# ScalarE instead of VectorE empties two PSUM banks of a deformable-convolution kernel

## The chip, the cores and the metric

The kernel runs on one core of a Trainium2 chip. The metric is the device time of one execution in microseconds, as the median of several runs. A core has five engines that run side by side and meet at semaphores: TensorE (PE in the profile) multiplies matrices into PSUM, VectorE (DVE) and ScalarE (ACT) do elementwise work and can read PSUM, GpSimd (POOL) does elementwise work on SBUF and issues transfers, SyncE (SP) issues transfers. Each engine works through its own list of instructions in order. All data here is float32.

## The reference

The input is 32 images of 96 x 56 x 56. Two layers follow each other.

Layer 0 is an inverted residual: a 1x1 convolution to 576 channels, batch norm and SiLU, a depthwise 3x3 convolution, batch norm and SiLU, a squeeze-and-excite gate, a 1x1 convolution back to 96 channels, batch norm, and the input added.

Layer 1 weighs its input by a channel attention and a spatial attention, both made from spectra and pooled statistics, and gets `y`. Then it computes, with `aux` made of `y`, coordinates and a resized spectrum:

```python
offset = _conv(aux, off_w, off_b, (1, 1))
gate = jax.nn.sigmoid(_conv(jax.nn.relu(_conv(aux, dg1_w, dg1_b, (1, 1))), dg2_w, dg2_b))
y_base = _conv(y, base_w, base_b, (1, 1))
...
sampled = _grid_sample_taps(y, px, py)
y_def = jnp.einsum('bcthw,oct->bohw', sampled, def_w.reshape(c, c, 9))
y_def = y_def + def_b[None, :, None, None]
z = (1 - gate) * y_base + gate * y_def
mu = z.mean((0, 2, 3), keepdims=True)
var = ((z - mu) ** 2).mean((0, 2, 3), keepdims=True)
...
return jax.nn.relu(zn + x)
```

`px` and `py` are the pixel's place plus the offsets of nine taps, and `_grid_sample_taps` samples bilinearly there. `zn` is `z` normalised over all images by `mu` and `var`.

## The kernel before

Layer 1 works in bands of 8 rows (448 pixels), seven per image, 224 in all. A band is made in two halves of seven tiles. Sampling is done by matrix products: for each 4 x 4 tile an 8 x 8 block of `y` is transposed (`block_channels`: GpSimd copies the blocks at L721, PE transposes at L725, ScalarE copies the result out at L727) and multiplied with a matrix of bilinear weights (`sample_tiles`: PE at L739, ScalarE copies to `v` at L743). `pack` (L750) copies the last two of the nine taps to the upper partitions on ScalarE, so that `deform` (L758) needs seven products per half. The products of both halves of a band go to one PSUM bank of a pool of its own, `pd`, with a single buffer. All other banks come from a pool of six, `mm` (a seventh, `acc`, serves small things).

`joint_conv` makes, in one bank of `mm`, the gate's hidden rows, the 18 rows of offsets and a third of the base convolution (nine products at L615); ScalarE empties the hidden rows (L635) and the base rows (L637), and the rest of the base convolution follows in another bank (L644, emptied at L649). `offsets` takes the offsets' rows out of the first bank with two copies, L664, to the tile `at`. GpSimd stores `at` to memory (L672), VectorE takes its largest magnitude (L676), SyncE loads it back spread over partitions, ScalarE turns it to weights (L687, L689), and VectorE multiplies row and column weights (`weights`, L710).

`end_half` issues the products of a half and, two slots after the second half, `join`: `combine` reads the `pd` bank and makes `z` with three VectorE steps (L797 to L799) and its statistics (L800); the store to memory (L1061, GpSimd) is issued seven slots later.

Beside a band, the generators of the other work are advanced by a fixed plan of slots (`pump`): layer 0 of the image after next (`hidden`: PE at L169, ScalarE at L173, and the depthwise convolution on VectorE, nine steps of up to 1568 columns at L260 and L262, then SiLU on ScalarE at L222), and projection and attention of the next image (among it the spectra: PE at L396 and L420, ScalarE at L423 and L427, VectorE's sums `m_fe` and `m_fy` at L437, and PE's products of these at L440). SyncE's list stands in the order of the program. On the other engines a scheduler places the instructions by its own estimate of times, so that a change of an engine can move others. After the last band `normalise` (L1347, L1349) runs through all of `z` once more. There is a second way of sampling for large offsets, `gather_block`, which also calls `combine`; the profile has no instruction of it.

Of the kernel before, what the change touches and what calls it, by code (L numbers as in the profile page):

```python
# [9 lines left out]
AF = mybir.ActivationFunctionType  # L10
ALU = mybir.AluOpType
# [5 lines left out]
C, H, W = 96, 56, 56  # L17
# [18 lines left out]
BW = NBW  # L36
TS = 4
NTX = W // TS
# [79 lines left out]
def bank(p):  # L118
    return p["mm"].tile([128, 512], FP, name="mm")
# [509 lines left out]
def joint_conv(nc, p, yp, j, hid):  # L629


    w = p["w"]
    pa = bank(p)
    conv3(nc, pa[:, :BW], w["joint"], yp, CJ, j)
    nc.scalar.activation(hid, pa[:DMID, :BW], AF.Relu, bias=w["dg1b"][:DMID])  # L635
    yb = p["yb"].tile([C, BW], FP, name="yb")
    nc.scalar.activation(yb[BC:], pa[OFF0 + QC :, :BW], AF.Identity, bias=w["cv"]("base_b")[BC:])  # L637
    yield yb, pa[OFF0 : OFF0 + NOFF, :BW]
    pb = bank(p)
    for k in range(NTAP):  # L640
        dy, dx = divmod(k, 3)
        r0 = j * RB + dy + PD - 1
        for i in range(2):
            nc.tensor.matmul(pb[i * BC : (i + 1) * BC, : BW // 2].rearrange("p (h w) -> p h w", h=RB // 2), w["base"][:, k],  # L644
                             yp[:C, r0 + i * RB // 2 : r0 + (i + 1) * RB // 2, dx + PD - 1 : dx + PD - 1 + W],
                             start=(k == 0), stop=(k == NTAP - 1))
    yield
    for i in range(2):
        nc.scalar.activation(yb[:BC, i * BW // 2 : (i + 1) * BW // 2], pb[i * BC : (i + 1) * BC, : BW // 2], AF.Identity,  # L649
                             bias=w["cv"]("base_b")[:BC])  # L650
    yield


def offsets(nc, p, yp, j, top, hid, ybs, hds, defer):

    w = p["w"]
    joint = joint_conv(nc, p, yp, j, hid)
    yb, pa = next(joint)  # L660
    ybs.append(yb)
    at = p["off"].tile([NOFF, NTX, 2, TP], FP, name="at")
    for s in range(2):
        nc.vector.tensor_copy(at[:, :, s].rearrange("o t (r c) -> o t r c", r=TS),  # L664
                              pa[:, s * BW // 2 : (s + 1) * BW // 2].rearrange("o (r t c) -> o t r c", r=TS, t=NTX))
    yield
    yield
    next(joint)
    yield
    od = p["dp"].tile([NTX, 2, NOFF, TP], FP, name="od")  # L670
    p["tc"].keep_in_program_order(
        nc.gpsimd.dma_start(od.rearrange("t s o p -> o (t s) p"), at.rearrange("o t s p -> o (t s) p")))  # L672
    next(joint)
    yield
    next(joint, None)
    nc.vector.tensor_reduce(top, at.rearrange("o t s p -> o (t s p)"), AX.X, ALU.max, apply_absolute_value=True)  # L676
    for _ in range(7):
        yield
    ht = p["ht"].tile([SB * NTX, 4, KP], FP, name="ht")
    src = od.rearrange("t s o p -> t (s o p)").unsqueeze(0).to_broadcast([SB, NTX, 4 * KP])  # L680
    nc.sync.dma_start(ht.rearrange("q n k -> q (n k)"), src)
    for _ in range(3):
        yield

    def hats():
        ho = p["ht"].tile([SB * NTX, 2, 2, KP], FP, name="ho")
        p["tc"].keep_in_program_order(nc.scalar.activation(  # L687
            ho.rearrange("q x s n -> q s x n"), ht.rearrange("q (s x) n -> q s x n", s=2), AF.Abs, bias=w["blk"]))
        nc.scalar.activation(ho, ho, AF.Relu, bias=w["one"], scale=-1.0)  # L689
        hd = p["dp"].tile([2, 2, SB, NTX, KP], FP, name="hd")  # L690
        nc.scalar.dma_start(hd.rearrange("x s i t n -> (i t) (x s) n"), ho.rearrange("q x s n -> q (x s) n"))
        hds.append(hd)

    defer(hats)
# [68 lines left out]
def gate_of(nc, p, hid):  # L763

    pg = bank(p)
    nc.tensor.matmul(pg[:C, :BW], p["w"]["dg2"], hid, start=True, stop=True)
    return gate_from(nc, p, pg)
# [17 lines left out]
def base_conv(nc, p, j, yp):  # L785

    pb = bank(p)
    conv3(nc, pb[:C, :BW], p["w"]["base"], yp, C, j)
    yb = p["q1"].tile([C, BW], FP, name="yb")
    nc.scalar.activation(yb, pb[:C, :BW], AF.Identity, bias=p["w"]["cv"]("base_b"))  # L790
    return yb


def combine(nc, p, j, pd, yb, gate, st):

    z = p["q2"].tile([C, BW], FP, name="z")
    nc.vector.scalar_tensor_tensor(z, pd[:C, :BW], p["w"]["cv"]("def_b"), yb, ALU.add, ALU.subtract)  # L797
    nc.vector.scalar_tensor_tensor(z, gate, 1.0, z, ALU.add, ALU.mult)
    nc.vector.scalar_tensor_tensor(z, z, 0.5, yb, ALU.mult, ALU.add)  # L799
    nc.vector.bn_stats(st[:, j], z)  # L800
    return z
# [152 lines left out]
def layers(tc, a, dp, x1d, zd, stats, far):  # L954
# [6 lines left out]
    nc = tc.nc  # L961
    B = x1d.shape[0]
    with ExitStack() as ctx:
        p = {"tc": tc, "dp": ctx.enter_context(tc.tile_pool(name="l1d", bufs=3, space=DRAM))}
# [3 lines left out]
        yp, = padded(nc, p, a, 1)  # L968
# [21 lines left out]
        streams, later = [], []  # L990
        slot = 0
# [68 lines left out]
        def store(b, j, z):  # L1060
            nc.gpsimd.dma_start(zd[b][:, j * BW : (j + 1) * BW], z)  # L1061

        def join(n, pd, gate, st):
            b, j = bands[n]
            z = combine(nc, p, j, pd, ybs[n], gate, st)
            later.append((slot + 7, lambda: store(b, j, z)))
            if j == NBD - 1:
                nc.vector.bn_aggr(stats[:, b], st)

        def end_half(n, h, v, gate, st):  # L1070
            if h == 0:
                pds[n] = p["pd"].tile([128, 512], FP, name="pd")
            deform(nc, p, pds[n], v, h)
            if h:
                pd = pds.pop(n)
                later.append((slot + 2, lambda: join(n, pd, gate, st)))

        ends, pds = [], {}

# [9 lines left out]
        hids, gates, ybs, hds, ready = [], [], [], [], []  # L1089
# [31 lines left out]
        for n, (b, j) in enumerate(bands):  # L1121
            if j == 0:
                st = p["st"].tile([C, NBD, 6], FP, name="st")
# [7 lines left out]
            for h in range(2):  # L1131
                v = p["vp"].tile([128, NTAP, NTH, 2, TP], FP, name="v")
                prepare(2 * n + h + READY + AHEAD)
                s = ready.pop(0)
# [17 lines left out]
                if h == 0:  # L1152
                    if n % 2 == 0:
                        gates.extend(gates_of(nc, p, hids[n // 2]))
                    gate = gates.pop(0)
# [108 lines left out]
def gather_block(tc, a, dp, x1d, zd, stats):  # L1264

    nc = tc.nc
    B = x1d.shape[0]
    sd = dp.tile([B, C, 2], FP, name="sd")
    with ExitStack() as ctx:
        p = {"dp": ctx.enter_context(tc.tile_pool(name="l1d", bufs=1, space=DRAM))}  # L1270
        pools(tc, ctx, p, PSUM, (("mm", 7), ("acc", 1)))
        constants(tc, ctx, a, p, True)
        yp, = padded(nc, p, a, 1)
        table = dp.tile([TAB, 4 * C], FP, name="table")
        with tc.tile_pool(name="l1z", bufs=1) as zp:
            zt = zp.tile([116, TAB * C // 116], FP, name="zt")
            nc.gpsimd.memset(zt, 0.0)
            tz = table.rearrange("(p n) f -> p (n f)", p=116)
            for i in range(4):
                nc.sync.dma_start(tz[:, i * zt.shape[1] : (i + 1) * zt.shape[1]], zt)  # L1280
        pools(tc, ctx, p, None, (("ca", 1), ("s1p", 1), ("xc", 2), ("sp", 1), ("sq", 2), ("hq", 1), ("q1", 2), ("q2", 2),
                                 ("hid", 2), ("off", 1), ("ix", 2), ("vp", 1), ("gp", 4), ("smp", 2)))
        with tc.For_i(0, B, 1) as b:
            st = p["sp"].tile([C, NBD, 6], FP, name="st")
            zo = p["dp"].tile([C, HW], FP, name="zo")
            xi = p["dp"].tile([C, HW], FP, name="xi")
            nc.sync.dma_start(xi.unsqueeze(0), x1d[bass.ds(b, 1)])
            for _ in attend(tc, p, 0, None, None, None, xi, True):
                pass
            for q in range(NB):  # L1290
                attend_table(nc, p, yp, table, xi, q)
            load_freq(nc, p, yp, 0, 0, H)
            for j in range(NBD):
                hid, wq, idx = locate(nc, p, yp, j)
                v = p["vp"].tile([C, NTAP, BW], FP, name="v")
                for t in range(GT):
                    sample_table(nc, p, table, wq, idx, v, t)
                pd = bank(p)
                for k in range(NTAP):
                    nc.tensor.matmul(pd[:C, :BW], p["w"]["def"][:, k], v[:, k], start=(k == 0), stop=(k == NTAP - 1))  # L1300
                z = combine(nc, p, j, pd, base_conv(nc, p, j, yp), gate_of(nc, p, hid), st)
                nc.sync.dma_start(zo[:, j * BW : (j + 1) * BW], z)
            mv = p["sp"].tile([C, 2], FP, name="mv")
            nc.vector.bn_aggr(mv, st)
            nc.sync.dma_start(zd[bass.ds(b, 1)], zo.unsqueeze(0))
            nc.sync.dma_start(sd[bass.ds(b, 1)].rearrange("o c n -> (o c) n"), mv)
    nc.sync.dma_start(stats, sd.rearrange("b c s -> c b s"))
# [209 lines left out]
```

## Time and profile before

| | us |
|---|---|
| median of 3 runs (lowest, highest) | 9049.27 (9045.97, 9068.44) |
| the profiled execution's own time | 9059.03 |
| span of the profiled execution | 9057.2 |
| PE busy | 8175.3 |
| VectorE busy | 7184.4 |
| ScalarE busy | 5393.5 |
| GpSimd busy | 2902.8 |

The page gives busy time per engine, the span in 40 slices (each digit is the busy share in tenths), the costliest groups of instructions by source line, and, behind the bar, the idle time of the engine just before the instructions of a group with what ended it. The view of waits adds these idle times up by engine, line and releaser. A matmul in float32 is recorded as two. PEclk is the clock that TensorE was granted, as a share of full speed; its mean over the execution was 0.939. In the slices of the middle the load is even: image follows image, one every 263 us or so.

### The profile page before, as it was taken

The numbers are of one execution on the slowest core, as the hardware profiler recorded it, in microseconds if no ns is written. First come the engines' busy times: TensorE is split into PE (matmuls) and PEld (weight loads), VectorE is DVE, ScalarE is ACT, GpSimd is POOL, SyncE is SP. The second block draws the span as 40 slices with busy tenths as digits, with TensorE's granted clock in tenths as the row PEclk, the third lists the DMA queues.
The fourth block names the chain that finished last, engine by engine and source line by source line (L and its number), as shares of the span: only waits on it lengthen the run. The fifth ranks groups of instructions, "written<-read, shape, count | busy, mean of one in ns | idle before, by whom it ended". The sixth has DMA issues, their size and how long they took to land. (4 is left out here: it accounts for less than half of the span.)

```text
span 9057.2 us, 137476 instructions
## 1 busy us (share of the span) xinstructions
PE 8175.3 (90%) x52406; PEld 5193.5 (57%) x52406; DVE 7184.4 (79%) x6629; ACT 5393.5 (60%) x10486; POOL 2902.8 (32%) x2800
## 2 busy tenths in 40 slices
PE   5889999999999999999999999999999999999960
PEld 3456565665656566565656656565665655566640
DVE  7688888888888888888888888888888888888333
ACT  2356665666666666666666666666666666666553
POOL 0233333333333333333333333333333333333210
PEclk9889999999999999999999999999999999999985
DMA  2356666666666666666666666666666666666669
GB/s 82 108 142 160 163 169 165 157 154 153 163 166 171 166 157 147 158 165 164 172 161 154 159 157 168 165 174 161 154 154 160 165 166 172 166 156 144 144 188 416
DMA packets 1068758, 1486.48 MB, mean 164 GB/s; under 512 B 590191, under 2 KB 839839, under 8 KB 1055807
## 3 DMA queue, kind: packets, MB, share of 16 engines
q1 hardware_dynamic: 858995, 985.20, 46.4%
q10 hardware_dynamic: 153803, 329.80, 10.2%
q0 software_dynamic: 55296, 162.60, 6.7%
q8 instruction: 420, 6.88, 0.4%
q14 instruction: 244, 1.99, 0.1%
HBM read 1064.29 MB, written 412.65 MB: 163 GB/s over the span
## 5 line engine op out<-in xcount | busy, mean ns | idle before, releaser
L262 DVE SCALAR_TENSOR_TENSOR acch<-hp,w,acch 128x1512 f32<-128x1512 f32 (+1 forms) x2250 | 4456.4, 1981 | 141.4 <-ACT hp L173 103.8
L615 PE MATMUL mm<-yp,c_jointW 104*128 104x448 f32 x4032 | 1679.6, 568 | 10.1 <-DMA yp<-fqd 10.1
L758 PE MATMUL pd<-v,c_def 128*96 128x224 f32 (+1 forms) x6272 | 1468.8, 382 | 142.7 <-DVE z L797 115.6
L721 POOL COPY ybl<-yp 96x448 f32<-96x448 f32 x896 | 1048.3, 1198 | 1204.9 <-PE mm L725 1204.8
L758 PEld LDWEIGHTS pd<-v,c_def 128*96 128x96 f32 (+1 forms) x6272 | 1062.2, 176 | 449.8 <-issue 116.9
L615 PEld LDWEIGHTS mm<-yp,c_jointW 104*128 104x128 f32 x4032 | 776.6, 196 | 784.2 <-issue 747.4
L743 ACT COPY v<-mm 96x288 f32<-96x288 f32 (+1 forms) x2688 | 1004.3, 441 | 156.0 <-PE mm L739 109.3
L169 PE MATMUL mm<-xt,w 96*128 96x392 f32 (+3 forms) x2688 | 1058.5, 527 | 35.3 <-DMA xt<-in_x 33.1
L739 PE MATMUL mm<-wc,yt 64*96 64x144 f32 x12544 | 1056.9, 300 | 20.8 <-DVE sq L379 6.7
L739 PEld LDWEIGHTS mm<-wc,yt 64*96 64x96 f32 x12544 | 834.2, 164 | 317.3 <-issue 199.1
L173 ACT ACTIVATE hp<-mm,sh,inv 128x392 f32<-128x392 f32 (+2 forms) x1216 | 810.7, 673 | 344.8 <-PE mm L169 290.5
L710 DVE TENSOR_TENSOR wc<-wc,wr 128x1008 f32<-128x1008 f32 x448 | 566.6, 1265 | 412.5 <-DMA wr<-hd 385.1
L644 PE MATMUL mm<-yp,c_base0W 96*64 96x224 f32 x8064 | 830.1, 358 | 5.7 <-ACT hp L173 5.7
L329 PE MATMUL mm<-hq,w3s 128*96 128x392 f32 x2048 | 749.7, 510 | 63.6 <-DMA hq<-h2d 62.2
L672 POOL DMA_DIRECT2D od<-at x224 | 186.7, 834 | 1908.3 <-DVE at L664 1292.6
L750 ACT COPY v<-v 32x448 f32<-32x448 f32 x1344 | 755.1, 562 | 29.7
L727 ACT COPY yt<-mm 128x384 f32<-128x384 f32 (+1 forms) x896 | 353.9, 439 | 700.7 <-PE mm L725 699.0
L644 PEld LDWEIGHTS mm<-yp,c_base0W 96*64 96x64 f32 x8064 | 555.2, 135 | 282.7 <-issue 61.0
L635 ACT ACTIVATE hid<-mm,c_dg1b 50x448 f32<-50x448 f32 x224 | 140.8, 628 | 868.4 <-PE mm L615 858.4
L476 POOL TENSOR_TENSOR o<-o,xc 96x392 f32<-96x392 f32 x256 | 376.2, 1470 | 806.2 <-ACT o L339 804.2
L222 ACT ACTIVATE acch<-acch,sh,inv 128x1568 f32<-128x1568 f32 x288 | 488.4, 1696 | 202.8 <-DVE acch L262 176.5
L329 PEld LDWEIGHTS mm<-hq,w3s 128*96 128x96 f32 x2048 | 323.0, 166 | 395.2 <-issue 367.5
(194 smaller groups left out, 9325.3 us busy)
## 6 DMA issues: line engine op xcount, KB each, us to landing
h2d<-acch ACTq DMA_DIRECT2D x288, 784.0 KB
wc<-hd SPq DMA_DIRECT2D x896, 252.0 KB
wr<-hd SPq DMA_DIRECT2D x448, 504.0 KB
hq<-h2d SPq DMA_DIRECT2D x128, 980.0 KB
hq<-h2d SPq DMA_DIRECT2D x128, 784.0 KB
hq<-x1d SPq DMA_DIRECT2D x768, 98.0 KB
ht<-od SPq DMA_DIRECT2D x224, 252.0 KB
hd<-ho ACTq DMA_DIRECT2D x224, 252.0 KB
```

What stands on the lines that cost most here:

```text
L169: nc.tensor.matmul(pt[p0 : p0 + w1.shape[1], : rows * W], w1, xts[hf][:, r0 * W : (r0 + rows) * W], start=True, stop=True)
L173: nc.scalar.activation(h1[lo:hi, row0 : row0 + rows, 1 : 1 + W], pt[lo:hi, : rows * W].rearrange("p (h w) -> p h w", h=rows), AF.Silu, bia ...
L262: nc.vector.scalar_tensor_tensor(acc[:, lo:hi], win, wk, acc[:, lo:hi], ALU.mult, ALU.add)
L329: nc.tensor.matmul(pts[half][:C, :EW], w3s[:, ch], hq, start=(i == 0), stop=False)
L615: nc.tensor.matmul(view, weights[:, k], yp[:channels, r0 : r0 + RB, dx + PD - 1 : dx + PD - 1 + W], start=(k == 0), stop=(k == NTAP - 1))
L644: nc.tensor.matmul(pb[i * BC : (i + 1) * BC, : BW // 2].rearrange("p (h w) -> p h w", h=RB // 2), w["base"][:, k], yp[:C, r0 + i * RB // 2 ...
L710: p["tc"].keep_in_program_order(nc.vector.tensor_tensor(wc, wc, wr, ALU.mult))
L721: nc.gpsimd.tensor_copy(yb[:, :, s], blocks)
L739: nc.tensor.matmul(pt[k][:C, (t - lo) * KP : (t - lo + 1) * KP], yt[ps, t], s[ps, t * KP : (t + 1) * KP], start=True, stop=True)
L743: nc.scalar.copy(v[:C, :, lo:hi, k].rearrange("c k t p -> c t k p"), pt[k][:C, : (hi - lo) * KP].rearrange("c (t k p) -> c t k p", t=hi - ...
L750: nc.scalar.copy(v[C:, 1 + 2 * i : 3 + 2 * i], v[i * QC : (i + 1) * QC, KA:])
L758: nc.tensor.matmul(out.rearrange("c q (t x) -> c t q x", x=TS), p["w"]["def"][ks, k], v[ks, k].rearrange("c t s (r x) -> c t (s r) x", r=T ...
```

## The change

Both places in which VectorE reads the results of layer 1 out of PSUM go to ScalarE.

The two copies of the offsets' rows (L664) become ScalarE copies of the same rows to the same tile. The first step of `combine`, which added the bias to the `pd` bank and subtracted the base convolution in one instruction, is split in two: a new function `take` copies the bank to `z` on ScalarE and adds the bias on the way, and `combine` begins with a subtraction on VectorE that reads and writes `z` in SBUF. `take` is called in `end_half` directly after the products of the second half, two slots before `join`; what `join` gets is `z`, not the bank. `gather_block` is changed in the same way.

```diff
     at = p["off"].tile([NOFF, NTX, 2, TP], FP, name="at")
     for s in range(2):
-        nc.vector.tensor_copy(at[:, :, s].rearrange("o t (r c) -> o t r c", r=TS),
-                              pa[:, s * BW // 2 : (s + 1) * BW // 2].rearrange("o (r t c) -> o t r c", r=TS, t=NTX))
+        nc.scalar.copy(at[:, :, s].rearrange("o t (r c) -> o t r c", r=TS),
+                       pa[:, s * BW // 2 : (s + 1) * BW // 2].rearrange("o (r t c) -> o t r c", r=TS, t=NTX))
...
-def combine(nc, p, j, pd, yb, gate, st):
+def take(nc, p, pd):
 
     z = p["q2"].tile([C, BW], FP, name="z")
-    nc.vector.scalar_tensor_tensor(z, pd[:C, :BW], p["w"]["cv"]("def_b"), yb, ALU.add, ALU.subtract)
+    nc.scalar.activation(z, pd[:C, :BW], AF.Identity, bias=p["w"]["cv"]("def_b"))
+    return z
+
+
+def combine(nc, p, j, z, yb, gate, st):
+
+    nc.vector.tensor_tensor(z, z, yb, ALU.subtract)
     nc.vector.scalar_tensor_tensor(z, gate, 1.0, z, ALU.add, ALU.mult)
     nc.vector.scalar_tensor_tensor(z, z, 0.5, yb, ALU.mult, ALU.add)
     nc.vector.bn_stats(st[:, j], z)
...
-        def join(n, pd, gate, st):
+        def join(n, z, gate, st):
             b, j = bands[n]
-            z = combine(nc, p, j, pd, ybs[n], gate, st)
+            combine(nc, p, j, z, ybs[n], gate, st)
...
             if h:
-                pd = pds.pop(n)
-                later.append((slot + 2, lambda: join(n, pd, gate, st)))
+                z = take(nc, p, pds.pop(n))
+                later.append((slot + 2, lambda: join(n, z, gate, st)))
```

More of the change, by code (lines that the diff above doesn't have):

```diff
@@ L1300, in gather_block @@
                     nc.tensor.matmul(pd[:C, :BW], p["w"]["def"][:, k], v[:, k], start=(k == 0), stop=(k == NTAP - 1))
-                z = combine(nc, p, j, pd, base_conv(nc, p, j, yp), gate_of(nc, p, hid), st)
+                z = take(nc, p, pd)
+                combine(nc, p, j, z, base_conv(nc, p, j, yp), gate_of(nc, p, hid), st)
                 nc.sync.dma_start(zo[:, j * BW : (j + 1) * BW], z)
```

## The prediction

> **What bounds the kernel now.** I read the page first (busy times, slices), then the waits of TensorE, then the groups of the moved lines, then the timeline around two gaps with the clock in narrow windows.
>
> ```profile
> span 9057.2 us, 137476 instructions
> PE 8175.3 (90%) x52406; PEld 5193.5 (57%) x52406; DVE 7184.4 (79%) x6629; ACT 5393.5 (60%) x10486; POOL 2902.8 (32%) x2800
> PE   5889999999999999999999999999999999999960
> ```
>
> From slice 4 to slice 38 PE is busy in nine tenths or more of every slice, and DVE in eight tenths. PE is the bound; what it still loses are waits, and this view lists them (who waited for what: us, times, longest):
>
> ```profile
> PE pd L758 <- DVE z L797: 115.6, 26, 6.1
> PE acc L440 <- DVE m_fy L437: 72.8, 30, 5.6
> PE acc L440 <- DVE m_fe L437: 71.1, 31, 2.5
> PE mm L725 <- DVE at L664: 57.2, 28, 5.7
> PE pd L758 <- ACT v L743: 19.3, 36, 2.8
> ```
>
> The first and the fourth row are what the change touches: about once per image PE stands before the next band's deformable products because VectorE has not yet emptied the single pd bank, and once before the transposes because the offsets' rows still hold a bank. The groups of the two lines, and of ScalarE's like-sized work:
>
> ```profile
> L797 DVE SCALAR_TENSOR_TENSOR z<-pd,c_cvec,yb 96x448 f32<-96x448 f32 x224 | 152.2, 679 | 170.3 <-PE pd L758 166.1
> L664 DVE COPY at<-mm 18x224 f32<-18x224 f32 x448 | 156.6, 380 | 201.8 <-ACT yb L637 197.8
> L637 ACT ACTIVATE yb<-mm,c_cvec 32x448 f32<-32x448 f32 x224 | 140.5, 627 | 4.1
> L649 ACT ACTIVATE yb<-mm,c_cvec 64x224 f32<-64x224 f32 x448 | 198.2, 443 | 320.7 <-PE mm L644 317.9
> ```
>
> One z gap, from the timeline, and the clock around it (the number before the last two columns is PEclk):
>
> ```profile
> 1040.09 6.78 DVE L262 SCALAR_TENSOR_TENSOR acch<-hp,w,acch 128x1568 f32<-128x1568 f32 x3
> 1042.71 1.74 ACT L750 COPY v<-v 32x448 f32<-32x448 f32 x3
> 1046.90 0.68 DVE L797 SCALAR_TENSOR_TENSOR z<-pd,c_cvec,yb 96x448 f32<-96x448 f32 x1
> 1047.64 1.06 PE L758 MATMUL pd<-v,c_def 96*96 96x224 f32 x2 [4.65 <-DVE z L797]
> ...
> 1043.00:1047.60 4.60, 0.00 (x0) 0.00 (x0) 4.48 (x4) 3.96 (x8) 0.00 (x0) 0.74 1.03 297
> 1047.60:1052.00 4.40, 4.36 (x14) 3.50 (x15) 4.25 (x8) 0.48 (x1) 0.52 (x1) 0.50 0.94 197
> 1052.00:1060.00 8.00, 8.00 (x61) 6.39 (x61) 5.48 (x7) 6.34 (x14) 1.06 (x2) 1.00 0.91 152
> ```
>
> The pd bank was full since 1037.9; z stood behind three 2 us steps of the first layer's depthwise convolution. PE then ran 4.4 us at half clock. A gap is thus paid twice.
>
> **The change, part by part.** I compared the built orders of both kernels. SP's is identical, PE's is the same at 27216 of 27773 places, POOL's in relative order at 2720 of 2801. ScalarE gains 672 instructions and no table load (130 in both); VectorE loses 448. On ScalarE each z copy stands behind nothing that PE finishes later, save one band per image with 1.4 us; the two offset copies stand right after L637. PE's first product of the next band no longer has a wait of its own for pd: the copy stands, on ScalarE, ahead of the v copies that the product awaits anyway.
>
> *A. The z gap.* 115.6 us in 26 gaps, at 4.4 us each. ScalarE can take the bank near 1038, since in this place it waited 2.25 us there. What is late next: the copies of L750, ending at 1044.45 where PE was free at 1043.0. The first product needs none of them, the others one by one; the added copy pushes them by up to 0.63. Ends: all 115.6 goes; or PE waits until 1045.1 in each, 2.1 of 4.4 us, and 60 goes. I take 100, nearer the upper end because the packed taps are used in order.
>
> *B. Half clock after it.* In windows of 1 us from 560 to 8780 I find half-clock stretches after every one of the 26 gaps; the busy time that they lost, window by window (1 minus PEclk, times busy), sums to 78 us. Ends 0 (shorter gaps still trip it: the one of 2.36 us that ends at 1360.1 is followed by 0.57 over 7 us) and 78. I take 60: most of the gaps vanish rather than shrink. The Trainium skill ("TensorE: Matmul & The Clock Gate", section on HAM oscillation) asks for no idle gap above about 3.4 us; 22 of the 26 are above, so by the page it would be 66, and the 2.36 us gap shows that shorter ones can cost too.
>
> *C. The offsets gap.* 57.2 us in 28. Here VectorE itself is behind, as this shows:
>
> ```profile
> 1454.32 0.69 DVE L664 COPY at<-mm 18x224 f32<-18x224 f32 x2
> 1455.04 0.61 DVE L676 TENSOR_REDUCE top<-at 18x1 f32<-18x448 f32 x1
> 1455.15 1.35 PE L725 MATMUL mm<-c_ident,ybl 96*128 96x96 f32 x7 [5.72 <-DVE at L664]
> 1455.58 1.59 DVE L436 TENSOR_TENSOR s<-s,cx 128x1392 f32<-128x1392 f32 x1
> 1457.20 2.57 DVE L437 TENSOR_REDUCE m_fy<-s 128x29 f32<-128x1392 f32 x1
> ```
>
> PE waits next for m_fy (L440), which VectorE reaches through the same queue. Without the two copies m_fy comes 0.69 us sooner; the rest of the gap moves to L440. 31 images by 0.69 is 21 us, which I take; ends 0 (L676 now waits for ScalarE's copies) and 57.2 (with the clock stretches there, up to 60 more).
>
> *D. ScalarE's new work.* z: 224 by 0.627 (L637) is 140 us. Offsets: a copy of 224 columns lies between the copy of 112 (L442, 0.23) and the ACTIVATE of 224 (L649, 0.443); copies of 288 take 0.403 (L727), so I take 0.35: 448 of them, 157 us (ends 103 and 198). Together 298, 1.33 us per band; ScalarE goes from 5393 to about 5690, 63%. Behind the offset copies stand two v copies of L743; behind z the yt copies of L727, for which ScalarE waited 699 us in all. The cover is this waiting (and 858 us at L635). PE's waits on ScalarE rows add up to 78 us now; ends of the charge are 0 and 298, I take 20, a quarter more waiting, since banks are freed with several us to spare. The Trainium skill ("ScalarE: Activation LUTs", rules for kernel authors) speaks against the move: adds belong on VectorE, an ACTIVATE costs about 0.3 us plus 0.83 ns per element. By that z would be 0.67 us, 150 us in all, against 140 by the row; it leaves out that here the waiting, not the duration, is paid.
>
> *E. VectorE.* It sheds 156.6 us. The z step becomes a plain subtraction from SBUF: between the tensor_tensor rows of 288 columns (L500, 0.446) and 1008 (L710, 1.265) lies 0.63 at 448, against 0.679: 11 us. L797's wait for PE (166 us) becomes one for ScalarE, later by the 0.63 of the copy: up to 64 by 0.63, 40 us, on VectorE alone, with the depthwise steps queued behind. Its idle time is some 41 us per image (421 of 500 us busy from 3000 on, and the z gaps recur every 263 us), so this costs PE nothing where the gaps above do not already say so. POOL's store of the offsets (L672, waiting 1292.6 us for L664) can go sooner, its landing was never waited for by PE. z's buffer is held two slots longer, of two buffers used once per band: nothing.
>
> Sum: 100 + 60 + 21 - 20 = 161 us off the profiled execution's 9059.0: 8898. That execution was 9.8 above the median of 9049.3, so 8888.
>
> **Rivals.**
> *VectorE holds the pace.* From 1163 to 1213 it has no idle time above 1 us; if PE, freed of the z gap, meets it again at the next result, half of A, B and C returns: 50 + 30 + 10 - 20 = 70 us, 8979 against the median. For: 85% busy in the middle stretches. Against: between 1213 and 1320 it waits some 29 us (eight waits above 1 us each), for PE, ScalarE and loads.
> *The gap changes hands.* ScalarE is itself late at the z gap (3.96 of 4.60 us busy), so PE waits as long for L750: only C - D remains, 9048: no change. Against: it waited 2.25 us just before.
> *Slower: ScalarE's added 1.33 us per band lands on PE*, because offset and z copies stand ahead of the yt and v copies that PE's next matmuls take. All of it gives 298 - 181 = 117 more, 9166. It decides from 181/298, 61% or 0.81 us per band. For: in-order queue, 63% busy, up to 99% in spots (7.90 of 8 us at 1056 and at 1088). Against: the built order, and 858 and 699 us of waiting just ahead of these places.
> That the change does not do what it says is excluded by the built order.
>
> **How the numbers follow.** Forecast 0.62, VectorE holds 0.20, gap changes hands 0.06, slower 0.12. About 0.3% (27 us) is what a measurement can tell from no change. Faster 0.82, same 0.06, slower 0.12. All upper ends give 115.6 + 78 + 117 = 311, 8738; I end the range at 8790, as not all come together. Upwards it must reach into the no-change case, 9030. The forecast's own range is 8790 to 8960.
>
> **What would show it.** Right: L758 waits for nothing of pd, half-clock stretches fewer by some 20, m_fy's row of L440 larger by up to 36 us while L725's row goes, VectorE near 7015 us, ScalarE near 5690. Wrong: new rows of PE waiting for L743, L727 or L750 of tens of us, or L440 and L739 waiting for VectorE by as much as z did.

## The result and the profile after

The changed kernel takes 9181.95 us (median of 4 runs, 9161.53 to 9199.14) against 9051.45 us for the kernel before beside it (9045.97 to 9068.44). The ratio is 1.014, with a 95% interval of 1.0115 to 1.0165. It is slower by 1.4%, where 1.8% faster was forecast. The profiled execution took 9182.1 us.

The head of the page of the changed kernel:

```profile
span 9180.3 us, 137679 instructions
PE 8190.3 (89%) x52406; PEld 5194.0 (57%) x52406; DVE 6976.1 (76%) x6181; ACT 5614.1 (61%) x11158; POOL 2939.7 (32%) x2800
```

VectorE is 208 us less busy and ScalarE 221 us more. TensorE's busy time hardly moved (8175.3 before), but the span grew by 123 us: TensorE waits longer. The view of TensorE's waits in the changed kernel (who waited for what: us, times, longest) says for whom; these are the rows that grew, and m_fe and m_fy:

```profile
PE mm L725 <- POOL ybl L721: 142.7, 14, 10.9
PE acc L440 <- DVE m_fe L437: 70.5, 31, 2.4
PE mm L739 <- DVE sq L379: 52.2, 30, 5.6
PE acc L440 <- DVE m_fy L437: 40.6, 15, 9.6
PE mm L615 <- DMA yp<-fqd: 38.8, 16, 4.7
PE mm L420 <- ACT hp L173: 33.5, 15, 3.3
```

The two rows that the change touches, L758 for z (115.6 us) and L725 for `at` (57.2 us), are gone. In their place stands a wait that the kernel before hardly had: the transposes wait for GpSimd's copies of the 8 x 8 blocks. It comes 14 times, about 10 us each. The same row before:

```profile
PE mm L725 <- POOL ybl L721: 1.0, 4, 0.3
```

The moved groups in the changed kernel (busy us, mean ns of one | idle time before them and what ended most of it):

```profile
L803 DVE TENSOR_TENSOR z<-z,yb 96x448 f32<-96x448 f32 x224 | 157.3, 702 | 278.9 <-ACT z L797 278.0
L797 ACT ACTIVATE z<-pd,c_cvec 96x448 f32<-96x448 f32 x224 | 140.4, 627 | 231.4 <-PE pd L758 230.3 <-ACT ho L689 0.5
L664 ACT COPY at<-mm 18x224 f32<-18x224 f32 x448 | 129.8, 336 | 2.6
```

(In the changed kernel L797 is `take`; `combine` is L803 to L806. Elsewhere the lines that are spoken of kept their numbers up to L791.) One of the 14 waits, in lines from the timeline of the changed kernel (start, us, engine, line, operation):

```profile
2224.98 11.94 POOL L373 TENSOR_TENSOR hq<-hq,sa 112x448 f32<-112x448 f32 x5
2231.09 7.43 DVE L262 SCALAR_TENSOR_TENSOR acch<-hp,w,acch 128x1568 f32<-128x1568 f32 x3
2236.87 0.54 POOL L596 DMA_DIRECT2D sab<-sad  x1
2237.40 0.85 POOL L672 DMA_DIRECT2D od<-at  x1
2238.27 1.23 POOL L373 TENSOR_TENSOR hq<-hq,sa 112x448 f32<-112x448 f32 x1
2239.45 0.55 POOL L596 DMA_DIRECT2D sab<-sad  x1
2240.58 0.66 SPq L681 DMA_DIRECT2D ht<-od  x1
2241.30 1.05 SPq L594 DMA_DIRECT2D yp<-x1d  x2
2246.10 0.68 DVE L602 SCALAR_TENSOR_TENSOR yp<-yp,ca,sab 96x448 f32<-96x448 f32 x1 [7.59 <-DMA yp<-x1d]
2247.08 0.51 POOL L596 DMA_DIRECT2D sab<-sad  x1 [7.07 <-DVE yp L602]
2247.58 7.00 POOL L721 COPY ybl<-yp 96x448 f32<-96x448 f32 x2
2254.63 1.38 PE L725 MATMUL mm<-c_ident,ybl 96*128 96x96 f32 x7 [10.87 <-POOL ybl L721]
```

Read it from the end. The transposes wait for the block copies (L721). These stand in GpSimd's list behind a third load of `sab` (the spatial attention spread over the channels, L596, in `load_rows`). `sab` has two buffers, so the third load waits for VectorE's L602, which multiplies the first of the next image's rows by its attention. L602 waits for those rows, whose load (L594) stands in SyncE's list behind the load of the offsets (L681). That one waits for the offsets' store (L672), which GpSimd issues only after five multiplications by the attention (L373). The place is the turn from one image to the next, once per image.

The kernel before has all of these instructions at the turn of the same image, in another order:

```profile
2215.04 0.68 DVE L797 SCALAR_TENSOR_TENSOR z<-pd,c_cvec,yb 96x448 f32<-96x448 f32 x1
2218.53 1.04 POOL L596 DMA_DIRECT2D sab<-sad  x2
2219.57 0.85 POOL L672 DMA_DIRECT2D od<-at  x1
2220.41 2.93 POOL L721 COPY ybl<-yp 96x448 f32<-96x448 f32 x2
2222.35 0.61 DVE L800 BATCH_NORM_STATS2 st<-z 96x6 f32<-96x448 f32 x1
2228.92 0.68 DVE L602 SCALAR_TENSOR_TENSOR yp<-yp,ca,sab 96x448 f32<-96x448 f32 x1 [5.96 <-DMA yp<-x1d]
2229.90 0.77 POOL L596 DMA_DIRECT2D sab<-sad  x1 [6.09 <-DVE yp L602]
```

Here too L602 waits for its rows, and the third `sab` load for L602, but the block copies and the four steps of `combine` stand ahead of them, and PE's wait for the block copies stays at the 1.0 us shown above, in the whole run. In the lists as built, over the 29 turns in the middle, L602 stands behind `combine` in every one of the kernel before and ahead of it in every one of the changed kernel; the third `sab` load stands ahead of the block copies in every second turn of the changed kernel, 14 times.

A half clock goes with such a wait too. The view of time windows of the changed kernel (us, then busy time of PE, PEld, DVE, ACT and POOL, then PEclk, DMA share and GB/s):

```profile
2243.80:2254.60 10.80, 0.00 (x0) 0.00 (x0) 8.50 (x10) 0.00 (x0) 7.52 (x4) 0.59 0.71 146
2254.60:2262.00 7.40, 7.37 (x53) 6.23 (x57) 7.26 (x5) 4.85 (x11) 5.05 (x4) 0.67 0.22 49
```

### The profile page after: what moved, and what is told of

Same layout as the page of the kernel before. It is cut to its first block, busy times and chain, and to the rows that moved or that the text cites. A ratio compares the mean times of both kernels' runs of the same rounds, so it can differ in the third digit from the quotient of the medians.

```text
span 9180.3 us, 137679 instructions
## 1 busy us (share of the span) xinstructions
PE 8190.3 (89%) x52406; PEld 5194.0 (57%) x52406; DVE 6976.1 (76%) x6181; ACT 5614.1 (61%) x11158; POOL 2939.7 (32%) x2800
## 5 line engine op out<-in xcount | busy, mean ns | idle before, releaser
L721 POOL COPY ybl<-yp 96x448 f32<-96x448 f32 x896 | 1141.9, 1302 | 1367.5 <-PE mm L725 1360.3
L758 PE MATMUL pd<-v,c_def 128*96 128x224 f32 (+1 forms) x6272 | 1385.3, 367 | 33.7 <-ACT v L743 32.4
L758 PEld LDWEIGHTS pd<-v,c_def 128*96 128x96 f32 (+1 forms) x6272 | 1017.0, 168 | 304.1 <-issue 80.3
L739 PE MATMUL mm<-wc,yt 64*96 64x144 f32 x12544 | 1085.9, 303 | 67.3 <-DVE sq L379 52.2
L743 ACT COPY v<-mm 96x288 f32<-96x288 f32 (+1 forms) x2688 | 1006.7, 443 | 107.8 <-PE mm L739 84.0
L739 PEld LDWEIGHTS mm<-wc,yt 64*96 64x96 f32 x12544 | 848.9, 165 | 372.1 <-issue 196.3
L710 DVE TENSOR_TENSOR wc<-wc,wr 128x1008 f32<-128x1008 f32 x448 | 598.8, 1337 | 541.2 <-DMA wr<-hd 497.7
L750 ACT COPY v<-v 32x448 f32<-32x448 f32 x1344 | 755.2, 562 | 29.6
L672 POOL DMA_DIRECT2D od<-at x224 | 186.4, 832 | 1391.9 <-ACT at L664 1342.8
L169 PEld LDWEIGHTS mm<-xt,w 96*128 96x128 f32 (+1 forms) x2688 | 364.9, 179 | 329.9 <-issue 229.0
```

What stands on the lines that cost most here:

```text
L169: nc.tensor.matmul(pt[p0 : p0 + w1.shape[1], : rows * W], w1, xts[hf][:, r0 * W : (r0 + rows) * W], start=True, stop=True)
L710: p["tc"].keep_in_program_order(nc.vector.tensor_tensor(wc, wc, wr, ALU.mult))
L721: nc.gpsimd.tensor_copy(yb[:, :, s], blocks)
L739: nc.tensor.matmul(pt[k][:C, (t - lo) * KP : (t - lo + 1) * KP], yt[ps, t], s[ps, t * KP : (t + 1) * KP], start=True, stop=True)
L743: nc.scalar.copy(v[:C, :, lo:hi, k].rearrange("c k t p -> c t k p"), pt[k][:C, : (hi - lo) * KP].rearrange("c (t k p) -> c t k p", t=hi - ...
L750: nc.scalar.copy(v[C:, 1 + 2 * i : 3 + 2 * i], v[i * QC : (i + 1) * QC, KA:])
```

## The experiments

Two theories were set against each other. *Order at the turn*: the scheduler, given the offsets on another engine, moved VectorE's L602 and GpSimd's third `sab` load forward at the turn, and what waits behind them is the loss. *ScalarE's added work lands on PE*: the third rival of the prediction, which gave 9166 us, close to what was measured.

To read the runs, the time from image to image is useful (between starts of L541 on PE, which comes once per image; means of 14 images each, the two kinds alternate). The ratios are those on record with their intervals; the quotient of two medians can differ from them by up to 0.0011:

| kernel | ratio to before, 95% interval | us per image, one kind / the other | PE's wait for L721, us |
|---|---|---|---|
| before | 1 | 262.4 / 266.7 | 1.0 |
| the change | 1.014 (1.0115 to 1.0165) | 263.5 / 274.1 | 142.7 |
| z part alone | 0.9927 (0.9911 to 0.9944) | 260.5 / 262.0 | 37.5 |
| offsets' part alone | 1.0048 (1.0031 to 1.0064) | 258.6 / 270.8 | 30.1 |
| change, band 5 on VectorE | 0.9859 (0.9838 to 0.988) | 257.1 / 261.7 | 17.2 |
| change, band 1 on VectorE | 1.0161 (1.0134 to 1.0188) | 262.0 / 274.2 | 136.6 |
| change, L602 kept late | 0.9927 (0.9911 to 0.9944) | 259.3 / 264.2 | 50.0 |
| change, third sab kept late | 1.0031 (1.0019 to 1.0043) | 263.7 / 266.1 | 0.3 |
| offsets' part, L602 kept late | 0.9946 (0.993 to 0.9963) | 258.9 / 266.8 | 51.0 |
| band 5 on VectorE, other copies twice | 0.9899 (0.9882 to 0.9915) | 259.2 / 261.7 | 22.6 |

The changed kernel lost almost nothing in one kind of image and 7.4 us in the other, the kind with the 14 waits.

**The two parts alone.** First the changed kernel with the offsets' copies back on VectorE:

```diff
-        nc.scalar.copy(at[:, :, s].rearrange("o t (r c) -> o t r c", r=TS),
+        nc.vector.tensor_copy(at[:, :, s].rearrange("o t (r c) -> o t r c", r=TS),
```

> Only the pd bank moves to ScalarE; the offsets' rows stay on VectorE. In the built order the third sab load (L596) stays behind the two block copies of L721 in all images, as in the kernel before. Theory 'GpSimd's order' (the changed kernel loses its time where, in every second image, the third sab load was placed ahead of the block copies and waits there for VectorE): no wait of PE for L721 (under 10 us in all), pd's wait for z gone, time at or below the kernel before, 8960 to 9050. Rival 'ScalarE's added work lands on PE': z is 140 of the 270 us that were added, so half of the loss, about 9110.

Measured: 8957.75 us against 9016.07, ratio 0.9927, 2 us under the range of the first theory. PE's wait for z is gone; its wait for L721 is 37.5 us in 43 short waits, not under 10. Then the kernel before with only this line changed the other way:

> Only the offsets' rows move to ScalarE; combine is as before. The built order puts the offsets' store two places earlier on GpSimd, but the third sab load stays behind the block copies in all images. Theory 'GpSimd's order': no wait of PE for L721 (under 20 us), the offsets' gap of 57 us gone, 9000 to 9060. Rival 'ScalarE's added work lands on PE': the offset copies are 130 of the 270 us that were added, so about 9110.

Measured: 9060.91 against 9016.07, ratio 1.0048: just above the range of the first theory and 50 us under the rival. The parts do not add up: -0.7% and +0.5% give +1.4% together. PE waits for L721 30.1 us, not under 20, and the loss is elsewhere. Lines from the timeline of the run with the offsets' part alone:

```profile
2202.13 7.42 DVE L262 SCALAR_TENSOR_TENSOR acch<-hp,w,acch 128x1568 f32<-128x1568 f32 x3
2216.41 0.68 DVE L602 SCALAR_TENSOR_TENSOR yp<-yp,ca,sab 96x448 f32<-96x448 f32 x1 [6.86 <-DMA yp<-x1d]
2217.01 0.68 DVE L797 SCALAR_TENSOR_TENSOR z<-pd,c_cvec,yb 96x448 f32<-96x448 f32 x1
2217.74 4.80 PE L758 MATMUL pd<-v,c_def 96*96 96x224 f32 x14 [5.59 <-DVE z L797]
```

L602 has moved forward here too, in every second image. The third `sab` load has not passed the block copies, but z, which VectorE still reads out of the single pd bank, stands behind L602. PE's wait for z grew from 115.6 us before to 172.2. The same move reaches PE by another way, which I had not foreseen in this expectation.

**The rows' load moved to ScalarE's queue**, in the changed kernel and, as a control, in the kernel before:

```diff
-    nc.sync.dma_start(rows, x1.rearrange("c (h w) -> c h w", h=H)[:, r0:r1])
+    nc.scalar.dma_start(rows, x1.rearrange("c (h w) -> c h w", h=H)[:, r0:r1])
```

> The changed kernel, but the loads of the next image's rows (L594) are issued by ScalarE, so that they no longer stand behind the load of the offsets (L681) in SyncE's list. The built order still has the third sab load ahead of the block copies, now in all images. Theory 'GpSimd's order, through L681 and the rows' load': VectorE's L602 comes sooner, the third sab load waits under 4 us, and PE's 142.7 us for L721 fall below 40: 9010 to 9080. If the sab load's place alone, and not the late rows, makes the wait: 300 us of PE waiting for L721 (31 images), 9300. Rival 'ScalarE's added work': no change, 9180.

> Control: the same move of L594 to ScalarE's queue in the kernel before. All theories: it moves no wait of PE that is in the list now, 9030 to 9070; a larger change would show what the place of this load is worth by itself, and is taken off the run beside it.

Measured: 9188.73 (ratio 1.0185) and 9176.19 (1.0168). The control missed: the kernel before becomes 1.7% slower by this move. PE's wait for ScalarE's L750 copies at L758, 3.3 us before, is 84.2 us in the control and 94.5 us in the changed kernel with the move. ScalarE's waits in the control say where it comes from (the kernel before has neither row; all of this idle time comes directly behind an L594 load):

```profile
ACT v L743 <- POOL ybl L721: 89.7, 30, 4.5
ACT v L750 <- POOL ybl L721: 82.1, 35, 4.2
```

In the built list the load carries a wait for GpSimd, whose block copies still read the tile that it writes. In SyncE's list this held up no copy of ScalarE; in ScalarE's list it holds up the copies behind it. Besides, the control does not keep the order: in its built lists, too, L602 stands ahead of `combine` and the third `sab` load ahead of the block copies, in each of the 29 turns. So the pair decides nothing. PE still waited 130.7 us for L721, in 34 waits, not under 40. That the change adds almost nothing on top of the control is noted, but with these side effects it is no proof.

**One band of seven back on VectorE.** In the changed kernel, with band 1 in the second run in the place of band 5:

```diff
-        nc.scalar.copy(at[:, :, s].rearrange("o t (r c) -> o t r c", r=TS),
+        (nc.vector.tensor_copy if j == 5 else nc.scalar.copy)(at[:, :, s].rearrange("o t (r c) -> o t r c", r=TS),
```

> The changed kernel, but in band 5 of each image, one of seven, VectorE copies the offsets' rows as before. In the built order this alone puts VectorE's L602 (the next image's rows) back behind the steps of combine, and GpSimd's third sab load back behind the block copies, as in the kernel with only the z part moved. Theory 'order at the turn' (the offsets' part costs by these two moves, which happen once per image): PE's 142.7 us for L721 fall below 45, time 8930 to 8990. Rival 'ScalarE's added work lands on PE': six sevenths of the offset copies are still on ScalarE, so six sevenths of what they cost on top of the z part remain: 9130 to 9160.

> Control with the same number of copies on each engine as in the run beside it: VectorE copies the offsets' rows in band 1 of each image. The built order at the turn stays that of the changed kernel (L602 ahead of combine, the third sab load ahead of the block copies in every second image). Theory 'order at the turn': PE still waits 130 to 150 us for L721, 9120 to 9180. Rival 'ScalarE's added work': the same time as with band 5, within 20 us.

Measured: 8902.23 with band 5 on VectorE (ratio 0.9859) and 9170.14 with band 1 (1.0161), against the same 9027.31. The first is 28 us under its range, the second within it. Both kernels give ScalarE the same number of copies. The built lists of PE, SyncE and GpSimd with band 1 are those of the changed kernel, instruction for instruction; with band 5 PE's differs from it at 8 of 28468 places and SyncE's not at all, but VectorE's and GpSimd's return to the old order at the turn. That is worth 268 us. Lines from the timeline with band 5 on VectorE, at the turn of the same image:

```profile
2175.26 7.42 DVE L262 SCALAR_TENSOR_TENSOR acch<-hp,w,acch 128x1568 f32<-128x1568 f32 x3
2182.61 1.55 DVE L803 TENSOR_TENSOR z<-z,yb 96x448 f32<-96x448 f32 x1
2184.49 4.34 POOL L721 COPY ybl<-yp 96x448 f32<-96x448 f32 x2
2190.33 0.61 DVE L806 BATCH_NORM_STATS2 st<-z 96x6 f32<-96x448 f32 x1
2191.31 0.68 DVE L602 SCALAR_TENSOR_TENSOR yp<-yp,ca,sab 96x448 f32<-96x448 f32 x1 [0.36 <-DMA yp<-x1d]
```

L602 follows `combine` and waits 0.36 us instead of 7.59. This version is the fastest of all, 1.4% faster than the kernel before, where the change as it was made is 1.4% slower.

**The order alone.** The band run still changes the engine of some copies. So the next two leave all of the change in place and tell the scheduler only to queue one instruction behind an earlier one of the same engine. First L602:

```diff
-                nc.vector.scalar_tensor_tensor(acc[:, lo:hi], win, wk, acc[:, lo:hi], ALU.mult, ALU.add)
+                p["lastdw"] = nc.vector.scalar_tensor_tensor(acc[:, lo:hi], win, wk, acc[:, lo:hi], ALU.mult, ALU.add)
...
-def attend_rows(nc, p, b, rows, sab):
+def attend_rows(nc, p, b, rows, sab, first=False):
-    nc.vector.scalar_tensor_tensor(rows, rows, p["ca", b], sab, ALU.mult, ALU.mult)
+    with p["tc"].issue_after(p["lastdw"].ins) if first else nullcontext():
+        nc.vector.scalar_tensor_tensor(rows, rows, p["ca", b], sab, ALU.mult, ALU.mult)
...
-                later.append((slot + 4, lambda args=args: attend_rows(nc, p, b, *args)))
+                later.append((slot + 4, lambda args=args, first=(r == 0 and b > 0): attend_rows(nc, p, b, *args, first=first)))
```

> The whole change, all copies on ScalarE, with one constraint for the scheduler: at the turn of each image the first L602 (the next image's rows) may not stand ahead of the last depthwise step that is traced before it. In the built order it stands behind combine's steps again, and the third sab load behind the block copies. Theory 'order at the turn': PE's 142.7 us for L721 fall below 45 and the time to that of the run with band 5 on VectorE or a little less, 8870 to 8930. Rival 'in band 5 ScalarE itself is too late' (that run was fast because ScalarE was spared the copies in this one band, not for the order): still 9100 or more.

Measured: 8978.69 against 9034.64, ratio 0.9927. This recovers 2.1 of the 2.8 points between the change and the band 5 run, with SyncE's list unchanged, PE's changed at 2 places and ScalarE's at 7; the rival's 9100 or more is excluded. The time missed its range by 49 us and the L721 row, 50.0 us, missed its 45. The constraint does not bring the old list back. In VectorE's built list the step for the image's first rows (L603 in this run) now stands seven depthwise steps behind `combine`, and the step for the second rows has passed it, to a place between the last two steps of `combine`. In the timeline the second rows' step comes first:

```profile
2199.16 0.68 DVE L603 SCALAR_TENSOR_TENSOR yp<-yp,ca,sab 96x448 f32<-96x448 f32 x1 [0.64 <-DMA yp<-x1d]
2216.88 0.68 DVE L603 SCALAR_TENSOR_TENSOR yp<-yp,ca,sab 96x448 f32<-96x448 f32 x1
```

Second, only the third `sab` load (in both kernels lines move by one: L740 is L739, L726 is L725):

```diff
-    nc.gpsimd.dma_start(sab, p["sa", b].rearrange("o (h w) -> o h w", h=H)[:, r0:r1].to_broadcast([C, r1 - r0, W]))
+    with p["tc"].issue_after(p["copies"][-5].ins) if r0 == 2 * RB and b else nullcontext():
+        nc.gpsimd.dma_start(sab, p["sa", b].rearrange("o (h w) -> o h w", h=H)[:, r0:r1].to_broadcast([C, r1 - r0, W]))
...
-        nc.gpsimd.tensor_copy(yb[:, :, s], blocks)
+        p.setdefault("copies", []).append(nc.gpsimd.tensor_copy(yb[:, :, s], blocks))
```

> The whole change, with the other half of the two moves undone alone: GpSimd's third sab load may not stand ahead of the block copies, while VectorE's L602 stays where the change put it, ahead of combine. Theory 'order at the turn', with GpSimd's list as the way to PE: the L721 row falls below 45 us and every second image takes as long as the other images of the changed kernel (264 instead of 274 us): 9182 - 14 x 10 = 9040, range 9000 to 9060. If VectorE's early L602 costs by itself as well, it stays over the run beside it by the rest. Rival 'ScalarE's added work': 9150 or more.

Measured: 9065.49 against 9034.64, ratio 1.0031, 5 us above its range. This is the smallest of the edits: the built lists of PE, VectorE, ScalarE and SyncE are those of the changed kernel, instruction for instruction, and GpSimd's differs at 42 of 3068 places, three in each of 14 turns. The wait for L721 is gone (0.3 us), and the bad kind of image falls from 274.1 to 266.1. With L602 still early, m_fy is what is late next. Rows of PE's waits in this run:

```profile
PE acc L440 <- DVE m_fy L437: 81.3, 27, 9.6
PE mm L740 <- DVE sq L379: 47.1, 30, 2.0
PE mm L420 <- ACT hp L173: 47.0, 29, 3.7
```

So the `sab` load's place is worth about one point (1.014 to 1.0031), and keeping L602 behind `combine` as well another (to 0.9927). The third run puts the L602 constraint on the offsets' part alone:

> Only the offsets' rows move to ScalarE (combine on VectorE as before), with the same constraint on L602. Theory 'order at the turn': here the early L602 had z behind it, so that PE waited 9.3 us per image for z in every second image, against 3.0 in the others; the constraint takes that back: z's row falls from 172 to about 100 us, time 8960 to 9020. Rival 'ScalarE's added work': no change from 9061.

Measured: 8993.12, ratio 0.9946 instead of 1.0048, and PE's wait for z falls from 172.2 to 108.2 us, near the 115.6 of the kernel before. The offsets' part alone is a gain once L602 stays behind `combine`.

**The price of ScalarE's work.** Two runs add work to the z part alone: copies of the offsets' rows that nobody reads (to a spare tile, made once), and a second take of the pd bank.

```diff
+        nc.scalar.copy(p["spare"].rearrange("o (t r c) -> o t r c", t=NTX, r=TS),
+                       pa[:, s * BW // 2 : (s + 1) * BW // 2].rearrange("o (r t c) -> o t r c", r=TS, t=NTX))
```

> Only the z part moved, and ScalarE copies the offsets' rows as well, to a spare tile that nobody reads (bfloat16), while VectorE's copies go on feeding everything: 448 copies of extra ScalarE work and nothing moved at the turn on GpSimd. This prices ScalarE's work by itself. Theory 'order at the turn': 0 to 30 us over the kernel with the z part alone, 8940 to 9000. Rival 'ScalarE's added work lands on PE': 130 us or more over it, 9090 or more.

```diff
     nc.scalar.activation(z, pd[:C, :BW], AF.Identity, bias=p["w"]["cv"]("def_b"))
+    nc.scalar.activation(z, pd[:C, :BW], AF.Identity, bias=p["w"]["cv"]("def_b"))
```

> Only the z part moved, and ScalarE's copy of the pd bank is made twice, to the same tile: 224 by 0.627, 140 us more on ScalarE, all of it between the last product of a band and the next band's first, and 0.63 us later for z on VectorE. Theory 'order at the turn' (ScalarE's work is covered): 0 to 40 us over the kernel with the z part alone, 8950 to 9000. Rival 'ScalarE's added work lands on PE': 140 us over it, 9100.

Measured: 9090.66 (ratio 1.0077) and 9015.76 (0.9989). The spare copies cost 133 us, as the rival said, but they do not price ScalarE's work, as this row of ScalarE's waits in that run shows:

```profile
ACT spare L666 <- DVE at L664: 605.5, 234, 6.9
```

ScalarE's copy waits for VectorE's copy of the same 18 rows, so ScalarE stood 605.5 us behind VectorE's copies. (The Trainium skill, "PSUM — Partial Sum Buffer", section "PSUM bank collisions raise a hardware error", tells of a compiler's scheduler that makes instructions of different engines depend on each other when they touch the same 32 partitions of one bank, two reads as well; this row shows such a wait of one reader for another.) The doubled take costs 58 us for 140, a miss of the upper bound, 40; its built order differs from that of the z part alone in VectorE's list at 615 of 7221 places, so part of this may be order again. The clean price came last, on the kernel with band 5 on VectorE:

```diff
-        (nc.vector.tensor_copy if j == 5 else nc.scalar.copy)(at[:, :, s].rearrange("o t (r c) -> o t r c", r=TS),
-                       pa[:, s * BW // 2 : (s + 1) * BW // 2].rearrange("o (r t c) -> o t r c", r=TS, t=NTX))
+        [copy(at[:, :, s].rearrange("o t (r c) -> o t r c", r=TS), pa[:, s * BW // 2 : (s + 1) * BW // 2].rearrange("o (r t c) -> o t r c", r=TS, t=NTX))
+         for copy in ((nc.vector.tensor_copy,) if j == 5 else (nc.scalar.copy, nc.scalar.copy))]
```

> The run with band 5's offset copies on VectorE, and every other copy of the offsets' rows made twice by ScalarE, to the same tile: 384 copies more, at 0.336 us (L664 in the changed kernel) 129 us of ScalarE work and nothing else; TensorE's and SyncE's built lists are the same instruction for instruction, VectorE's and GpSimd's but for a few neighbours. This prices ScalarE's work with the order held. The prediction's charge (20 us for 298) makes it 9 us; the rate of the doubled z copy (58 us for 140, with a changed order) makes it 53: ratio to the kernel before 0.987 to 0.992. Rival 'ScalarE's added work lands on PE': all 129, ratio 1.000.

Measured: 8935.28 against 9027.66, ratio 0.9899. The kernel without the second copies had 0.9859; the difference of 0.0040 is 36 us for 129, and the two intervals together (0.0017 and 0.0021) leave 12 to 60. About 28% of ScalarE's added time is paid, the rest is covered. The lists of PE and SyncE are the same in both kernels, GpSimd's differs at 6 places and VectorE's at 122 of 6837. The rival's 129 is excluded, and the prediction's charge, 9, lies just below the interval. How the 36 us are paid is not shown: all listed waits of PE are 11.3 us per image in both kernels, and it is PE's busy time that is longer, 8142.5 us against 8114.5.

## Why the prediction was wrong

**The step that failed is the reading of the built order.** The prediction says "SP's is identical, PE's is the same at 27216 of 27773 places, POOL's in relative order at 2720 of 2801", and goes on to count durations. VectorE's list, from which the change takes 448 instructions, is only counted ("VectorE loses 448"). The places that differ were never looked at: among them were the third `sab` load ahead of the block copies in 14 images, and L602 ahead of `combine` in 29. In step E this stands as "POOL's store of the offsets ... can go sooner, its landing was never waited for by PE". Its landing was waited for by a chain that ends at PE: L681, L594, L602, `sab`, L721. The row in which this showed, L725 waiting for GpSimd, is none of those that the prediction named as signs of being wrong. With this order undone the change is worth 0.9927 (by a constraint) or 0.9859 (by one band of seven on VectorE); the forecast, 8888 against 9049, was 0.982.

Why the scheduler moved them is argued, not shown: offsets that it expects sooner make it expect the rows sooner, since their load stands behind the offsets' on SyncE. Shown is that the engine of band 5's two copies decides it, and that at the turn above the rows came 7.59 us after VectorE was ready.

By the steps:

*A, the z gap, taken at 100 us.* The row vanished, but most of the gain was taken up by others. With the z part alone, the view of PE's waits has

```profile
PE mm L739 <- DVE sq L379: 51.3, 28, 2.3
PE mm L615 <- DMA yp<-fqd: 38.2, 21, 5.2
PE mm L725 <- POOL ybl L721: 37.5, 43, 3.1
PE mm L396 <- DVE sq L379: 20.9, 18, 2.4
```

Of these, the first was 6.7 us before, the second 10.1, the third 1.0. All waits of PE fell from 14.3 to 12.7 us per image (the 28 images of the table), some 50 us in 31 images: the lower end, 60, was nearer. A good part of this is the rival "VectorE holds the pace": two of the four rows wait for VectorE's sums.

*B, the half clock, taken at 60 us.* Summed in the same way (windows of 1 us, here from 560 to 8660), the loss is 322 us before and 256 with the z part alone: 67 us, near the 60 taken. In the changed kernel it is 306: the new gaps brought most of it back. The 50 and the 67 us are differences of single profiled executions, and that of the kernel before (9059.03 us) is 43 us above the median beside the z part's run, so they may be too large: by the medians the z part gained 58 us.

*C, the offsets' gap, taken at 21 us.* Too small, and with the sign of one row wrong. I expected L440's row for m_fy to grow by up to 36 us; with the offsets' part alone and L602 late it fell from 72.8 to 21.3 us, by more than the copies' own time would give (21 us); VectorE's order changed as well, and the two were not separated. The gap at the transposes changed hands: 57.2 us for VectorE's copies became 51.0 us for GpSimd's block copies. That run gained 0.54% (42 us by the medians), with its share of D paid.

*D, ScalarE's work.* 270 us were added (140.4 and 129.8 of busy time; 298 was predicted). z took exactly the 627 ns of L637, an offset copy 336 ns instead of 350, and some of the copies overlap. The charge of 20 us was too small: the measured 28%, applied to all of it, makes it an estimated 76. The Trainium skill ("ScalarE: Activation LUTs", rules for kernel authors) puts adds on VectorE. Here the take with the bias add on ScalarE gained 0.7%: it took 627 ns against the 679 of VectorE's step, and PE's 115.6 us of waiting for z went.

*E, VectorE's relief.* VectorE's busy time was predicted near 7015 and came to 6976.1. The subtraction from SBUF was taken at 630 ns; its mean is 702, above the 679 of the step out of PSUM. The mean hides two groups. The view of these lines (ns, least/median/most):

```profile
L803 DVE TENSOR_TENSOR z<-z,yb x224: 602/621/987, 486.4 to 8891.5; 96x448 f32<-96x448 f32 x112
L797 DVE SCALAR_TENSOR_TENSOR z<-pd,c_cvec,yb x224: 665/680/690, 487.1 to 8768.5; 96x448 f32<-96x448 f32 x112
```

The first is the changed kernel, the second the kernel before. In the changed kernel 64 of the 224 subtractions took over 700 ns, each while GpSimd was working, nearly always at its block copies; the other 160 took 616 ns in the mean. So the estimate held for an undisturbed subtraction, and what it left out is GpSimd beside it.

Of the rivals, "ScalarE's added work lands on PE" gave 9166 us, 16 from the measured time, by a mechanism that the band 5 and doubled-copy runs exclude as the main one. A number that fits is not a cause.

What stays open: why the L602 constraint alone (0.9927) falls 0.7 points short of band 5 on VectorE (0.9859). The largest single difference in PE's waits is L721's row, 50.0 against 17.2 us. Whether that comes from the constraint's own effect, which puts the first rows' step later than it was in the kernel before and moves GpSimd's list, or from ScalarE's two copies in band 5 was not separated. A third `sab` buffer, which would take the third load's wait away, was not tried.

## What to carry to other kernels

Where a scheduler orders the engines' lists, a move of work between engines is two changes: the durations, and the order. Compare the lists of all engines, and for each instruction that stands earlier than it did, ask what it waits for on the hardware and who stands behind it. Here it waited for a load that stands behind another load in SyncE's list. When a change that should gain loses in every second period, look at the order in the bad period before blaming the engine that got the work.

## What the runs showed of the hardware that I had not expected

A VectorE step that reads two SBUF tiles can be lengthened by GpSimd's work beside it. In the changed kernel the subtraction L803 (96 x 448, float32) took at most 633 ns where GpSimd was idle and up to 987 ns where it worked. The step before it in the kernel before, L797, which reads one operand out of PSUM, took 665 to 690 ns whether GpSimd worked or not.

A load brings its wait into the list of the engine that issues it. With the 224 row loads in ScalarE's list instead of SyncE's, ScalarE waited 171.8 us for GpSimd's block copies ahead of L743 and L750, PE's wait for L750 rose from 3.3 to 84.2 us, and the kernel before lost 1.7%. How much of that the waits took, and how much the order that changed with them, was not separated.

Gaps of PE of 1.93, 2.00, 2.38 and 3.14 us ahead of L758 in the kernel before were each followed by 3 to 6 us at a granted clock of 0.50, where the 4 us ahead of them had 1.00.
